# A decoder layer on one core: weights stored in four parts, score copies shared by two engines, and extra products on TensorE in the first batch

## The chip, the cores and the metric

The kernel runs on one core of one Trainium2 chip. The metric is device time in microseconds, the median of several executions. The core has a matrix engine (PE, with its weight loads shown as PEld), a vector engine (DVE), a scalar engine (ACT), GpSimd (POOL) and a sync engine (SP). Each engine takes its own instructions in their order and waits on semaphores where it needs another one's result. SP, ACT and POOL also issue transfers (SPq, ACTq, POOLq in the profile). Matrix results go to PSUM, from which DVE or ACT must copy them before anything else can use them.

## The reference: what is computed

Eight batches of 512 tokens by 256 channels in float32 pass through one decoder layer:

```python
x = _layernorm(x + attn(x))                  # banded self-attention, 16 heads of 16 channels
x = _layernorm(x + xattn(x, ctx, ctx))       # causal cross-attention
x = _layernorm(x + ffn(x))                   # 8 experts, the best 2 for each token
# attn:
q = _ln(silu(x @ Wq)); k = _ln(silu(x @ Wkv)[..., :C]); v = silu(x @ Wkv)[..., C:]
wp = silu(x @ Wwin + bwin)                   # gives a width and a sharpness per token and head
scores = stack([einsum('blhd,blhd->blh', q, k_pad[:, w:w+L]) for w in range(17)]) * SCALE
soft_mask = sigmoid((width - rel) * sharp)
attn = softmax(scores - (1.0 - soft_mask) * 1e4)
out = silu(sum(attn[..., w] * v_pad[:, w:w+L] for w in range(17)) @ Wout)
```

Every token sees 17 neighbours in the self-attention. The experts are two matrices with a gelu between them, 256 to 1024 to 256 channels.

## The kernel before

**Stages.** The work on a batch falls into three streams. `scores(b)` makes the projections, the layer norms of q and k, and the raw scores. `attended(b)` does the softmax, the weighted sum of values and the output projection. `crossed(b)` does the cross-attention and the routing to experts. The main loop runs from -2 to 8 and lays `crossed(b)`, `attended(b + 1)` and `scores(b + 2)` beside each other, so in the first round there is only `scores(0)`, in the second `scores(1)` and `attended(0)`, and in the third all three. From the fourth round on, tiles of the experts (`experts`) fill in: one tile in the fourth round, eight in the fifth, and so on. A function called `together` interleaves the streams by the amounts that they yield. From this, the framework's scheduler sets an order for PE, DVE, ACT and POOL by its own estimate of durations, so an edit at one place can move other instructions on those engines. The order on SP is that of the program.

**Scores (lines 309 to 430).** The batch is transposed on PE (line 248) and copied to `xT` by ACT (257). For each of four 128-token tiles PE makes two projections: `pa` (q and k, line 321) and `pb` (v and the window inputs, line 322). ACT copies them out through a silu (323, 324), and DVE adds the bias of the window inputs to `wp` (325). `wp` passes ACT twice (328, 334), goes to DRAM (335) and comes back in another layout as `ws` (POOL, 395), from which DVE builds the mask input `pen` (474, 485, 491) and ACT its sigmoid (492). Meanwhile q and k are normed (342 to 356), transposed (367) and copied to `qT` and `kT` (372, 378).

Then PE makes the scores `pq` (line 413) in four groups: two halves of the channels (c) by two pairs of token tiles (ip). A group has 16 products into four PSUM buffers, one per row group r. ACT copies the four buffers into `row` (421), which has two buffers, and issues two transfers of `row` to the DRAM tensor `band[c]` (425). The scores of half c come back as `s[c]` in the layout of one token quadruple per partition (`read_scores`, line 387, on POOL).

```python
                for r in range(HG):
                    nc.scalar.copy(row[:, :, r], pq[r])
```

**Weighted sums of the first three batches (`summed`, lines 495 to 588; `BANDED` is 3).** For each half c: DVE adds `pen` to `s` (518), takes the maximum (525) and subtracts it (526), ACT takes the exponential (529), and DVE sums and divides (531 to 533). The weights then go to the DRAM tensor `aband[c]` in one transfer (537) from SP: partition p holds tokens 4p to 4p + 3, in pieces of 136 bytes. They come back by groups of 128 tokens (`fetch`, 506, two transfers each, into two buffers `arow`). Group g reads the tokens that partitions 32g to 32g + 31 stored. PE transposes a group (`paT`, 575), DVE and ACT copy it to `aT` (579), PE multiplies it with the values (`pw`, 553), and ACT and DVE put the halves together in `oT` (562, 563). For c = 0 the first two fetches stand right behind the store on SP; each later one waits until PE has read the group two before it. From the fourth batch on another routine (`weighted`) does this part on DVE.

**The rest that the prediction speaks of.** `py` (595) is the output projection and `y` its silu (603). The norm that follows ends in DVE's `off` (292) and four scalings on ACT (295). In the cross-attention the transposes of `xr` and `c` give `x1T` and `cT` (248, 257); the scores `ps` (711), the softmax (718 to 727), the transposes `pt` (700) and the sums `po` (685) follow in steps. `route` ends in eight scatters to `sorted_x` (815) from POOL. An expert tile starts with the load `xs` from `sorted_x` (942, SP), which waits for all scatters of the batch, and its transpose `pxs` (997) on PE.

Of the kernel before, what the change touches and what calls it, by code (L numbers as in the profile page):

```python
# [8 lines left out]
F32 = mybir.dt.float32  # L9
# [5 lines left out]
P = 128  # L15
L = 512
E = 256
# [3 lines left out]
W = 17  # L21
# [4 lines left out]
HG = HH // 2  # L26
LINE = HG * SPAN * 2
HALO = W // 2
T = L // P
# [8 lines left out]
BANDED = 3  # L38
# [6 lines left out]
def decoder_layer_kernel(  # L45
# [16 lines left out]
    nc = tc.nc  # L62
# [4 lines left out]
    last = N // TS  # L67
# [10 lines left out]
    ps_h = ctx.enter_context(tc.tile_pool(name="ps_h", bufs=2, space=PSUM))  # L78
# [15 lines left out]
    wall = cpool.tile([P, KC, 3 * E + 2 * H], F32, name="wall")  # L94
# [4 lines left out]
    ident = cpool.tile([P, P], F32, name="ident")  # L99
# [75 lines left out]
    scattered, adds, out_of, read, turns, urgent = [], [], {}, [], [], []  # L175
# [112 lines left out]
    def layernorm(a, last=False, by=None):  # L288
# [4 lines left out]
        for j in range(T):  # L293
# [5 lines left out]
            else:  # L299
# [2 lines left out]
                    ALU.mult, ALU.add,  # L302
                )

    def scores(b, xb):


# [7 lines left out]
        for t in range(T):  # L315
            pa = ps_m.tile([P, 2 * E], F32, tag="m", name="pa")
            pb = ps_m.tile([P, E + 2 * H], F32, tag="m", name="pb")
            for kc in range(KC):
                lhs = xT[:, kc, t * P : (t + 1) * P]
                se = dict(start=(kc == 0), stop=(kc == KC - 1))  # L320
                nc.tensor.matmul(pa, lhs, wall[:, kc, 0 : 2 * E], **se)  # L321
                turns.append(nc.tensor.matmul(pb, lhs, wall[:, kc, 2 * E :], **se))  # L322
            nc.scalar.activation(qk[:, t, :], pa, AF.Silu)  # L323
            nc.scalar.activation(v[:, t, :], pb[:, 0:E], AF.Silu)
            nc.vector.tensor_tensor(wp[:, t, :], pb[:, E:], bwin_sb, ALU.add)  # L325
            yield 0.8
        yield 8.4
        nc.scalar.activation(wp, wp, AF.Silu)
        for c in range(2):
# [54 lines left out]
        def read_scores(c):  # L384
            lines = band[c].rearrange("(p t n) -> p t n", p=P, t=T)[:, :, 0:LINE]
            read.append(
                nc.gpsimd.dma_start(  # L387
                    s[c].rearrange("p t r w u -> p t r (w u)"),
                    lines.rearrange("p t (r n) -> p t r n", r=HG)[:, :, :, 0 : 2 * W],
                )  # L390
            )
# [9 lines left out]
        for c in range(2):  # L401
            s.append(apool.tile([P, T, HG, W, 2], F32, tag="s", name="s", bufs=3))
            for ip in range(T // 2):
                row = apool.tile([P, 2, HG, SPAN, 2], F32, tag="row", name="row", bufs=2)
                pq = [
                    ps_m.tile([P, 2, SPAN, 2], F32, tag="m", name=f"pq{r}") for r in range(HG)
                ]
                for ii in range(2):
                    for u in range(2):
                        at = (2 * ip + ii) * P + u * QB  # L410
                        for r in range(HG):
                            rs = slice(32 * r, 32 * r + 32)
                            nc.tensor.matmul(  # L413
                                pq[r][u * QB : (u + 1) * QB, ii],
                                qT[rs, c, at : at + QB],
                                kT[rs, c, :, at : at + SPAN].rearrange("p u k -> p k u"),
                                start=True,
                                stop=True,
                            )
                for r in range(HG):  # L420
                    nc.scalar.copy(row[:, :, r], pq[r])  # L421
                to = band[c].rearrange("(b n) -> b n", b=L // QB)[:, 0 : QB * LINE]
                to = to.rearrange("(i u) (p n) -> u p i n", u=2, n=LINE)
                for u in range(2):
                    nc.scalar.dma_start(
                        to[u, :, 2 * ip : 2 * ip + 2],
                        row[u * QB : (u + 1) * QB].rearrange("p i r k u -> p i (r k u)"),
                    )
                yield 2.0

                if c == 1 and ip == 0:
                    read_scores(0)
# [48 lines left out]
        for c in range(2):  # L481
            pc = pen[:, c].rearrange("p t r w u -> p (t r) w u")
            wc = width[:, c].rearrange("p t (r u) -> p (t r) u", u=2)
            sc = sharp[:, c].rearrange("p t (r u) -> p (t r) u", u=2)
# [11 lines left out]
    def summed(b):  # L496


        groups = [(c, g) for c in range(2) for g in range(T)]
        rows_of = {}  # L500

        def fetch(c, g):
            ar = apool.tile([P, HG, SPAN, 2], F32, tag="a", name="arow", bufs=2)
            for u in range(2):
                ub = (g * P + u * QB) * (LINE + 2)
                nc.sync.dma_start(
                    ar[u * QB : (u + 1) * QB].rearrange("p r k u -> p (r k u)"),
                    aband[c][ub : ub + QB * LINE].rearrange("(p n) -> p n", p=QB),
                )
            rows_of[c, g] = ar  # L510

        s, pen, vh = out_of.pop(b)
        for c in range(2):
            sc = s[c]


            with tc.issue_after(urgent[-1].ins) if urgent and c == 0 else nullcontext():
                nc.vector.scalar_tensor_tensor(
                    sc, pen[:, c], -4.0e4, sc, ALU.mult, ALU.add
                )  # L520
            flat = sc.rearrange("p t r w u -> p (t r) w u")
            byw = sc.rearrange("p t r w u -> p (t r) u w")
            full = [P, T * HG, W, 2]
            top = spool.tile([P, T * HG, 2], F32, tag="top", name="top")
            nc.vector.tensor_reduce(top, byw, AX.X, ALU.max)
            nc.vector.tensor_tensor(
                flat, flat, top[:, :, None, :].to_broadcast(full), ALU.subtract
            )
            nc.scalar.activation(sc, sc, AF.Exp, scale=0.25)
            den = spool.tile([P, T * HG, 2], F32, tag="den", name="den")  # L530
            nc.vector.tensor_reduce(den, byw, AX.X, ALU.add)
            nc.vector.reciprocal(den, den)
            nc.vector.tensor_tensor(
                flat, flat, den[:, :, None, :].to_broadcast(full), ALU.mult
            )
            lines = aband[c].rearrange("(p t n) -> p t n", p=P, t=T)[:, :, 0:LINE]
            nc.sync.dma_start(
                lines.rearrange("p t (r n) -> p t r n", r=HG)[:, :, :, 0 : 2 * W],
                sc.rearrange("p t r w u -> p t r (w u)"),
            )  # L540
            if c == 0:

                for early in groups[:2]:
                    fetch(*early)
            yield 5.0
        oT = apool.tile([P, KC, L], F32, tag="T", name="oT", bufs=4)
        aT = apool.tile([P, 2, HG, 2, P], F32, tag="prod", name="aT")

        def sums(c, g):
            po = ps_o.tile([P, 2, 2, QB], F32, tag="o", name="pw")  # L550
            for u in range(2):
                for r in range(HG):
                    nc.tensor.matmul(
                        po[32 * r : 32 * r + 32, u],
                        vh[c][0:SPAN, 2 * g + u, 32 * r : 32 * r + 32],
                        aT[0:SPAN, g % 2, r, :, u * QB : (u + 1) * QB],
                        start=True,
                        stop=True,
                    )

            to = oT[:, c, g * P : (g + 1) * P].rearrange("c (u q) -> c u q", u=2)
            nc.scalar.mul(to, po[:, :, 0, :], par[:, 0:1])
            nc.vector.scalar_tensor_tensor(
                to, po[:, :, 1, :], par[:, 1:2], to, ALU.mult, ALU.add
            )

        for k, (c, g) in enumerate(groups):
            if 2 <= k + 1 < len(groups):
                fetch(*groups[k + 1])
            ar = rows_of.pop((c, g))  # L570
            for i in range(2):
                pt = ps_h.tile([P, 2, 2, P], F32, tag="h", name="paT")
                for r in range(2):
                    for u in range(2):
                        nc.tensor.transpose(  # L575
                            pt[0:SPAN, r, u, :], ar[:, 2 * i + r, :, u], ident
                        )
                put = nc.scalar.copy if i else nc.vector.tensor_copy
                put(aT[0:SPAN, g % 2, 2 * i : 2 * i + 2], pt[0:SPAN])
            if k:  # L580
                sums(*groups[k - 1])
            yield 1.4
        sums(*groups[-1])
        yield 0.8
        return oT
# [616 lines left out]
```

## Time and profile before

| what | value |
|---|---|
| median of 3 runs | 1038.47 us (1036.89 to 1040.36) |
| the profiled execution's own time | 1045.55 us |
| its span, first to last instruction | 1043.8 us |
| mean granted clock of PE | 0.913 |
| PE busy over the span | 916.5 us (88%) |
| DVE, ACT, POOL busy | 627.4, 556.7, 251.5 us |
| 0 to 48 us (`scores(0)` alone) | PE 27.43 us busy, DVE 17.86, ACT 23.89, clock 0.77 |
| 48 to 107 us (second round) | PE 43.70, DVE 29.33, ACT 33.31, clock 0.76 |
| 107 to 204 us (third round) | PE 86.16, DVE 57.64, ACT 60.61, clock 0.80 |
| 204 to 300 us (fourth round) | PE 77.10, DVE 54.69, ACT 57.92, clock 0.79 |
| 300 to 1000 us (expert tiles) | PE 670.97, DVE 450.84, ACT 364.72, clock 0.98 |

The profile shows one execution. Times in a timeline are microseconds from the start of the span; its columns are start, duration, engine, line, operation, output and inputs, and in brackets the idle time of that engine before it with what ended it. The clock is the share of PE's full speed that it was granted. A group "x32" of PE in the timeline counts records: a float32 product shows as two records, a transpose as one. The bounds of the rounds are read off the timeline; the rounds overlap by a few us.

### The profile page before, as it was taken

The page shows a single profiled execution, that of the slowest core. Times are in us where ns is not written, and L with a number is a line of the kernel's source. Part 1 is how long each engine was busy: PE and PEld are TensorE (multiplying, and loading weights), DVE is VectorE, ACT ScalarE, POOL GpSimd, SP SyncE. Part 2 cuts the span into 40 slices and gives each one's busy share as a digit, 9 for nine tenths or more (in the row PEclk, how much of TensorE's full clock was granted, in tenths as well). Part 3 has the DMA queues.
Part 4 walks back from the last instruction along what each step waited for, and adds up shares of the span by engine and source line. Part 5 has one row for each costly group of instructions (what it writes and reads, how often), then busy time and mean ns, then how long its engine had stood idle before and what let it go on. Part 6 is the DMA issues. An engine that isn't in the chain of part 4 may idle for free. (4 is left out here: it accounts for less than half of the span.)

```text
span 1043.8 us, 18932 instructions
## 1 busy us (share of the span) xinstructions
PE 916.5 (88%) x6336; PEld 761.6 (73%) x6336; DVE 627.4 (60%) x2106; ACT 556.7 (53%) x978; POOL 251.5 (24%) x211
## 2 busy tenths in 40 slices
PE   5658879868979999999999999999999989999970
PEld 3435557546858777777888778887998988999960
DVE  5164654754489969979994989489953331111106
ACT  4556746656467556658755865576355311222224
POOL 1100100400232243125212522152241241121221
PEclk9677877867799989999999999999999999999995
DMA  9574563872699788689978896898898899999949
GB/s 205 137 124 135 115 153 81 227 164 64 185 319 311 239 267 271 198 257 337 282 206 268 309 292 184 234 364 292 264 279 256 272 260 372 314 337 323 330 116 320
DMA packets 129123, 252.09 MB, mean 242 GB/s; under 512 B 29536, under 2 KB 76704, under 8 KB 127744
## 3 DMA queue, kind: packets, MB, share of 16 engines
q1 hardware_dynamic: 89312, 183.30, 54.3%
q0 software_dynamic: 17824, 41.86, 16.2%
q10 hardware_dynamic: 21888, 25.70, 9.0%
q8 instruction: 52, 0.85, 0.3%
q14 instruction: 47, 0.39, 0.1%
HBM read 193.44 MB, written 57.36 MB: 240 GB/s over the span
## 5 line engine op out<-in xcount | busy, mean ns | idle before, releaser
L1011 PEld LDWEIGHTS ph<-xsT,w1h 128*128 128x128 f32 x2176 | 264.6, 196 | 14.2 <-issue 5.2
L1011 PE MATMUL ph<-xsT,w1h 128*128 128x128 f32 x2176 | 271.6, 280 | 2.9 <-DVE xsT L1000 2.8
L1028 PE MATMUL pf<-w2h,h 128*128 128x256 f32 x1088 | 255.9, 386 | 3.2 <-ACT h L1019 3.1
L1028 PEld LDWEIGHTS pf<-w2h,h 128*128 128x128 f32 x1088 | 204.1, 194 | 32.0 <-ACT h L1019 5.7
L1037 POOL DMA_INDIRECT total<-ye,toi x68 | 120.4, 1771 | 417.0 <-ACT ye L1036 117.0
L1019 ACT ACTIVATE h<-ph 128x512 f32<-128x512 f32 x136 | 81.2, 598 | 119.0 <-PE ph L1011 115.0
L1000 DVE COPY xsT<-pxs 128x256 f32<-128x256 f32 x68 | 28.7, 423 | 174.6 <-PE pxs L997 174.6
L651 DVE TENSOR_TENSOR prod<-prod 128x1024 f32<-128x1024 f32 (+3 forms) x160 | 104.1, 651 | 0.3
L1036 ACT ACTIVATE ye<-pf,g 128x256 f32<-128x256 f32 x68 | 32.2, 473 | 127.2 <-PE pf L1028 116.7
L643 DVE TENSOR_TENSOR prod<-vhalo,a 128x2176 f32<-128x2176 f32 x40 | 96.6, 2416 | 0.2
L815 POOL DMA_INDIRECT sorted_x<-xr,to x64 | 78.2, 1222 | 19.9 <-issue 17.1
L413 PE MATMUL pq<-kT,qT 32*64 32x160 f32 x1024 | 60.3, 391 | 19.2 <-ACT row L421 12.7
L387 POOL DMA_DIRECT2D s<-band x16 | 24.3, 1520 | 214.5 <-DMA band<-row 154.5
L321 PE MATMUL pa<-wall,xT 128*128 128x512 f32 x128 | 67.5, 615 | 6.0 <-ACT qk L323 4.7
L413 PEld LDWEIGHTS pq<-kT,qT 32*64 32x64 f32 x1024 | 37.2, 156 | 33.8 <-ACT row L421 18.1
L421 ACT COPY row<-pq 128x320 f32<-128x320 f32 x128 | 45.8, 435 | 29.4 <-PE pq L413 26.6
L575 PE MATMUL paT<-ident,arow 128*80 128x128 f32 x192 | 38.0, 346 | 20.0 <-DMA arow<-aband 17.1
L1019 ACT ACT_TABLE_LOAD x39 | 50.0, 1283 | 7.3 <-PE ph L1011 5.7
L322 PEld LDWEIGHTS pb<-wall,xT 128*128 128x128 f32 x128 | 24.2, 192 | 35.3 <-issue 23.0
L575 PEld LDWEIGHTS paT<-ident,arow 128*80 128x80 f32 x192 | 26.2, 167 | 30.8 <-issue 13.0
L711 PE MATMUL ps<-cT,x1T 128*128 128x128 f32 (+3 forms) x128 | 45.5, 476 | 0.0
L322 PE MATMUL pb<-wall,xT 128*128 128x288 f32 x128 | 41.3, 410 | 3.9 <-DVE wp L325 1.6
(196 smaller groups left out, 1392.4 us busy)
## 6 DMA issues: line engine op xcount, KB each, us to landing
w1h<-in_w_dram SPq DMA_DIRECT2D x136, 512.0 KB
w2h<-in_w_dram SPq DMA_DIRECT2D x136, 512.0 KB
band<-row ACTq DMA_DIRECT2D x64, 320.0 KB
vhalo<-vband POOLq DMA_DIRECT2D x10, 1280.0 KB, 10.1
xs<-sorted_x SPq DMA_DIRECT2D x68, 132.5 KB
arow<-aband SPq DMA_DIRECT2D x48, 160.0 KB
s<-band POOLq DMA_DIRECT2D x16, 272.0 KB, 5.8
xr<-in_x_dram SPq DMA_DIRECT2D x8, 512.0 KB
```

The costliest lines, as they stand in the source:

```text
L321: nc.tensor.matmul(pa, lhs, wall[:, kc, 0 : 2 * E], **se)
L322: turns.append(nc.tensor.matmul(pb, lhs, wall[:, kc, 2 * E :], **se))
L413: nc.tensor.matmul(pq[r][u * QB : (u + 1) * QB, ii], qT[rs, c, at : at + QB], kT[rs, c, :, at : at + SPAN].rearrange("p u k -> p k u"), st ...
L421: nc.scalar.copy(row[:, :, r], pq[r])
L575: nc.tensor.transpose(pt[0:SPAN, r, u, :], ar[:, 2 * i + r, :, u], ident)
L643: nc.vector.tensor_tensor(prod.rearrange("p w (h d) -> p w h d", d=D), vh[c][:, t : t + W, :].rearrange("p w (h d) -> p w h d", d=D), a[:, ...
L651: nc.vector.tensor_tensor(prod[:, 0:n, :], prod[:, 0:n, :], prod[:, n : 2 * n, :], ALU.add)
L815: sent = nc.gpsimd.indirect_dma_start(out=sorted_x[:, :], out_offset=bass.IndirectOffsetOnAxis(ap=to[:, n, j : j + 1], axis=0), in_=xr[:, ...
L1011: nc.tensor.matmul(ph[:, u, :], w1s[hf][:, kc, f * P : (f + 1) * P], xT[:, kc, :], start=(kc == 0), stop=(kc == KC - 1),)
L1019: nc.scalar.activation(h, ph, AF.Gelu)
L1028: nc.tensor.matmul(po, hs[fc // HU][:, fc % HU, j * P : (j + 1) * P], w2s[hf][:, f, :], start=(fc == 0), stop=(fc == NF - 1),)
L1037: add = nc.gpsimd.indirect_dma_start(out=total[:, :], out_offset=bass.IndirectOffsetOnAxis(ap=toi[:, j : j + 1], axis=0), in_=y, in_offset ...
```

## The change

It has three parts, and the order that the scheduler gives to PE, ACT and DVE in the first four rounds differs with them. The order on POOL is the same; SP has the added transfers and is otherwise the same. From the routing in the fourth round on, the order of every engine is the same as before.

1. The store of the weights of half c = 0 becomes four stores of 32 partitions each, so that a group's fetch depends on the one store that holds its tokens. The store of half c = 1 stays whole.
2. For the first three batches the four copies of a score group are shared: r = 0 and 2 on ACT, r = 1 and 3 on DVE.
3. In the first batch PE gets products that nothing reads: six of a 128x128 by a 128x512 operand behind the last projection, and one behind each score group.

```diff
+    def hold(n, behind):
+
+        none = ps_h.tile([P, 2 * E], F32, tag="h", name="none")
+        with tc.issue_after(behind.ins):
+            for _ in range(n):
+                nc.tensor.matmul(none, ident, wall[:, 0, 0 : 2 * E], start=True, stop=True)
...
             yield 0.8
+        if b == 0:
+            hold(6, turns[-1])
         yield 8.4
...
-                            nc.tensor.matmul(
+                            last = nc.tensor.matmul(
...
+                if b == 0:
+                    hold(1, last)
                 for r in range(HG):
-                    nc.scalar.copy(row[:, :, r], pq[r])
+                    put = nc.vector.tensor_copy if b < BANDED and r % 2 else nc.scalar.copy
+                    put(row[:, :, r], pq[r])
...
-            nc.sync.dma_start(
-                lines.rearrange("p t (r n) -> p t r n", r=HG)[:, :, :, 0 : 2 * W],
-                sc.rearrange("p t r w u -> p t r (w u)"),
-            )
+
+            parts = T if c == 0 else 1
+            for ps in (slice(k * P // parts, (k + 1) * P // parts) for k in range(parts)):
+                nc.sync.dma_start(
+                    lines[ps].rearrange("p t (r n) -> p t r n", r=HG)[:, :, :, 0 : 2 * W],
+                    sc[ps].rearrange("p t r w u -> p t r (w u)"),
+                )
```

## The prediction, made before the changed kernel was run

> **What bounds the kernel now.** First the busy shares of the page (PE 88%), then busy time by rounds. Columns: bounds, length, busy us of PE, PEld, DVE, ACT, POOL, clock, DMA share, GB/s.
>
> ```profile
> 0.00:48.00 48.00, 27.43 (x190) 18.17 (x191) 17.86 (x39) 23.89 (x45) 5.19 (x26) 0.77 0.73 168
> 48.00:107.00 59.00, 43.70 (x372) 27.71 (x371) 29.33 (x55) 33.31 (x62) 4.22 (x6) 0.76 0.63 134
> 107.00:204.00 97.00, 86.16 (x545) 59.10 (x546) 57.64 (x210) 60.61 (x118) 16.78 (x16) 0.80 0.56 133
> 204.00:300.00 96.00, 77.10 (x543) 56.06 (x541) 54.69 (x193) 57.92 (x108) 16.24 (x16) 0.79 0.62 174
> 300.00:1000.00 700.00, 670.97 (x4622) 590.53 (x4623) 450.84 (x1521) 364.72 (x615) 200.13 (x139) 0.98 0.89 282
> ```
>
> After 300 us PE is busy 671 of 700 at clock 0.98, and the order there is the same in both kernels, so a shift at 300 us arrives at the end one to one. Everything is decided before it, where chains leave PE idle 20.6, 15.3, 10.8 and 18.9 us a round at clocks below 0.8. The timeline shows the chains that the change touches:
>
> ```profile
> 36.10 1.11 ACT L492 ACTIVATE pen<-pen 128x1088 f32<-128x1088 f32 x1 [2.99 <-DVE pen L491]
> 37.12 1.39 ACT L421 COPY row<-pq 128x320 f32<-128x320 f32 x4
> 46.48 1.54 POOL L387 DMA_DIRECT2D s<-band  x1 [14.77 <-DMA band<-row]
> ...
> 57.83 0.60 SPq L537 DMA_DIRECT2D aband<-s  x1
> 67.19 2.44 SPq L506 DMA_DIRECT2D arow<-aband  x4
> 70.96 1.91 PE L575 MATMUL paT<-ident,arow 128*80 128x128 f32 x8 [7.49 <-DMA arow<-aband]
> 72.06 0.69 DVE L579 COPY aT<-paT 80x512 f32<-80x512 f32 x1 [4.17 <-PE paT L575]
> 72.67 0.18 DVE L325 TENSOR_TENSOR wp<-pb,bwin_sb 128x32 f32<-128x32 f32 x1
> 72.88 0.31 ACT L328 ACTIVATE wp<-wp 128x128 f32<-128x128 f32 x1 [5.77 <-DVE wp L325]
> ...
> 124.72 0.63 SPq L537 DMA_DIRECT2D aband<-s  x1
> 131.26 2.75 SPq L506 DMA_DIRECT2D arow<-aband  x4
> 136.01 0.84 PE L575 MATMUL paT<-ident,arow 128*80 128x128 f32 x3 [4.85 <-DMA arow<-aband]
> ...
> 210.12 0.67 SPq L537 DMA_DIRECT2D aband<-s  x1
> 217.51 2.40 SPq L506 DMA_DIRECT2D arow<-aband  x4
> 221.52 1.91 PE L575 MATMUL paT<-ident,arow 128*80 128x128 f32 x8 [3.08 <-DMA arow<-aband]
> ```
>
> Store to first fetch takes 9.36, 6.54 and 7.39 us, and PE, DVE and ACT all stand idle for it near 71. Windows on the second store:
>
> ```profile
> 124.70:126.00 1.30, 1.30 (x6) 0.72 (x5) 1.30 (x6) 1.14 (x2) 0.00 (x0) 1.00 0.00 0
> 126.00:128.40 2.40, 2.40 (x9) 1.29 (x8) 2.40 (x7) 2.32 (x6) 0.00 (x0) 1.00 0.85 116
> 128.40:131.20 2.80, 1.66 (x12) 1.13 (x10) 2.80 (x7) 1.68 (x5) 0.00 (x0) 1.00 0.00 0
> ```
>
> The DMA engines are idle 1.3 us, move 2.4, and are idle again for 2.9 until the fetch.
>
> **Part 1, the products.** A 128x512 product takes 0.86 us at full clock (starts of successive projections 9.73 and 10.59). Six behind the last projection (its end 19.3) take 5.2 us and end at 24.5, inside PE's 6.08 us of idle before the transposes of q and k at 25.38. At half clock they take 10.3, and the transposes start 4.2 late. Both are covered: the row copies wait on ACT behind the sigmoid of `pen` (36.10), which waits for a load that POOL can issue only at 30.92, while the first two groups end at 32.7. A clock kept up speeds the transposes (3.76 us for 16 records) by at most 1.9, for the same reason worth nothing. If the cover were gone, the six would cost 0 to 4.2. The single ones cost 0.86 or 1.72 each; behind the second group the wait of ACT for a free `row` (43.26) covers it, behind the last one PE goes to transposes that `xT` on ACT needs. Together 0 to 0.65, I take 0.3.
>
> **Part 2, the copies.** Four copies of a group take 1.39 to 1.41 us on ACT; two take 0.75 (another row of the trace has that pair). DVE's 128x320 copy from PSUM is not in the trace; the nearest rows are 128x256 in 0.42 and 80x512 in 0.69, so about 0.5 each, 1.0 the pair, 0.85 to 1.4 as bounds. PSUM buffers come free two at a time, so PE's third group of 16 products (37.58) can start some 0.6 to 1.0 earlier, and each of the two remaining groups saves 0.4. DVE idles there (17.86 of 48 busy). The read of `s` at 46.48 moves up by about 1.3; minus the 0.3, first round **-1.0** (0 to -1.5). Later rounds: DVE is busy 29 of 59 and 58 of 97, ACT 33 and 61; a copy waits behind whatever DVE does, so I take nothing, bounds -0.6 to +0.6 a round.
>
> **Part 3, the stores.** SP issues four transfers for one: 4 x 0.63 = 2.5 us, 1.9 more, while SP only waits for the fetch, whose first part needs the first store alone. By the windows, part 0 needs 1.3 us to its first packet, a quarter of 2.4 = 0.6 moving, and 0.7 to 2.9 to be seen: 2.6 to 4.8. I take 4.0, since the end looks like latency; gain 2.5 (1.7 to 3.9) per store, for the first of 9.36 more, to about 5. The later groups wait for two `arow` buffers, so they are not bound by parts 2 and 3 (issued 1.3 and 1.9 later). The second half's store, 69.80, queues behind the fetches on SP and moves with them.
>
> A price for splitting, beside the row: the Trainium skill, page "DMA: Bandwidth & Descriptors", section "Rules for kernel authors", says to coalesce, since under 64 KB one mostly pays overhead; the parts are 68 KB. By its fit in "Anatomy of one DMA" (2.0 us and bytes over 436,000, for another issue path) whole and part differ only 2.6 to 2.2 us: my estimate by that page is 0.5 per store. The row here, 6.5 to 9.4 us for the whole, is far above that fit, so the measurement decides; the rule is rival 1.
>
> **What follows in each round**, with the changed order of the instructions.
> - Second (48 to 107). The order puts `wp` of the last tile and the norms of q and k ahead of the first `aT` copy on DVE, so the `scores(1)` chain no longer waits for the fetch: `wp` 72.67 to about 66.8, the first row copies 96.48 to 90.5, the read of `s` 106.36 to 98.7. Of that 1.0 is round one, the store about 3, and the rest the reordering: **-7.0** (-2.5 to -8). If `wp` were still behind `aT`, only the -3 is left.
> - Third (107 to 204). The store at 124.72 moves to about 115.6. PE's idle 4.85 before 136.01 is filled with the scores and sums of the cross-attention, which the new order puts ahead of `paT`. Against it: ACT does `y2`, `cT`, `xT` ahead of the exponential, about 1.4. Then PE is the limit (22.41 of 24 us at 145 to 169, 20.32 of 21 at 169 to 190), so what was idle is the whole gain: **-1.5** (0 to -4). The load `xs` at 209.67, behind the scatters, would come at about 200.
> - Fourth (204 to 300). PE's order now has `pxs` (211.84, waits for `xs`) ahead of the transposes of `xr` that ran at 204.38; queued behind it are `x1T`, `ps` and `paT`. That costs about 2.8 (transposes 1.97, a copy 0.58), and the store here gives 2.5 of PE's 3.08 idle before 221.52: **0** (-0.4 to +2.8).
>
> Sum: -1.0 -7.0 -1.5 + 0 = **-9.5**. The profiled execution took 1045.55 (span 1043.8 and 1.75 around it), 7.1 above the median; it becomes 1036.05, and the median 1038.47 becomes **1029.0**.
>
> **Rivals.**
> 1. *Only the stores help, or little of them.* If a part takes as long as the whole, the latency being fixed, the stores give about 0; the reordering near 72 is what remains, -4.5 in all: 1034. For it: 2.9 of 6.54 us pass with idle DMA engines. Against: 6.54, 7.39 and 9.36 differ, so something grows with load.
> 2. *The clock stays up.* Two half-clock stretches lie before 300:
>
> ```profile
> 145.00:169.00 24.00, 22.41 (x216) 16.18 (x215) 20.83 (x62) 17.56 (x36) 0.02 (x1) 0.99 0.32 94
> 169.00:190.00 21.00, 20.32 (x169) 15.44 (x170) 4.11 (x22) 12.69 (x28) 2.21 (x2) 0.51 0.63 151
> 248.00:275.00 27.00, 25.17 (x235) 19.20 (x236) 4.85 (x22) 14.43 (x33) 2.01 (x2) 0.57 0.41 109
> ```
>
>    If filled gaps kept half of the 20 us from 169 at full clock, 5 more are saved: -14.5, 1024. The stretch was cold with PE busy 97%. The Trainium skill, page "TensorE: Matmul & The Clock Gate", Part 1, has the clock released after about 3.4 us of sustained activity and gated after an idle window; by that rule 169 to 190 would have been warm, which the row denies, so it earns only a small chance.
> 3. *Slower: the hot stretch goes cold.* The new order moves score products, transposes and router products, among which PE ran at half clock here, into the third round's filled gap, and 145 to 169 (22.41 us of PE at 0.99) may lose its clock. All of it cold adds 20 or so: 1038.47 - 9.5 + 20 = 1049. It decides from some 10 us of bound PE work turned cold. For it: clock changes come in blocks of 3.4 us whatever the busy share. Against: most of that stretch's work is 512 wide and unchanged.
> 4. *No change.* The lead is used up at the first barrier, the scatters to `xs`, or by 2.8 in the fourth round on top of a second round of -3: 1038. For it: barrier waits hide early finishes; against: the last scatter hangs on the same chain that moves up.
>
> **How the numbers follow.** Forecast 0.50 (its own range 1024 to 1033: the sums of the bounds, narrowed as they won't all fall together); rival 1 0.19, rival 2 0.10, no change 0.08, slower 0.13. About 0.3%, 3.1 us, is what a measurement here can tell from no change. Faster by more: 0.50 + 0.19 + 0.10 less 0.01 for rival 1's near edge = 0.78; same 0.09; slower 0.13. The range 1020 to 1037.5 leaves out the slower case and a part of no change, 2 in 10.
>
> **What would show it.** Six unread products end before 25.4; two DVE row copies a group, of about 0.5; the first fetch 4 to 5 us after its store's first issue; `wp` L328 no longer waiting some 5.8 us on DVE; `paT` waits near 71 and 136 shrunk by half or gone; `xs` issued near 200; PE from 300 on shifted by one number only. Wrong if fetches still come 6.5 us behind, if clocks in 107 to 300 fall below 0.79, or if `pxs` holds PE longer than 3 us more.

## The result and the profile after

The changed kernel was timed four times beside the kernel before. The lower the ratio, the faster the changed kernel.

| timing | changed, median | before, median | ratio, 95% interval |
|---|---|---|---|
| first, 22 executions of each | 1035.99 us | 1040.86 us | 0.9957 [0.9936, 0.9978] |
| `changed_again`, 12 against 35 | 1045.90 | 1050.46 | 0.9973 [0.9940, 1.0007] |
| `changed_third`, 6 against 18 | 1026.38 | 1038.34 | 0.9908 [0.9874, 0.9942] |
| `changed_fourth`, 12 against 23 | 1042.36 | 1047.56 | 0.9959 [0.9928, 0.9990] |

The ratio leaves out the executions in a slower state and is not the quotient of the two medians, which take in all.

Weighted by the inverse squares of the half widths the four give 0.9952, with a half width of 0.0014: about 5 us faster. The second and the third lie further apart than their intervals allow, so this half width is too small. Forecast were 9.5 us, 0.0091. The sign was right and the size twice too large. The kernel before timed against itself gave 0.9976 [0.9938, 1.0015] (`before_third`), so differences of two or three thousandths between two runs below mean little.

The profiled execution of the changed kernel took 1032.45 us, its span is 1030.8. Against the profile of before that is 13.1 us less, more than twice the difference of the medians: one pair of profiles does not give the size of this change. Busy time by rounds in the changed kernel (columns as in the prediction):

```profile
0.00:48.00 48.00, 37.73 (x214) 20.09 (x215) 21.36 (x47) 21.85 (x38) 5.95 (x26) 0.86 0.72 172
48.00:107.00 59.00, 42.74 (x385) 29.07 (x384) 32.70 (x63) 33.00 (x57) 5.04 (x6) 0.80 0.73 151
107.00:204.00 97.00, 77.82 (x531) 52.29 (x529) 67.63 (x226) 61.26 (x111) 16.52 (x16) 0.88 0.57 136
204.00:300.00 96.00, 80.26 (x599) 60.31 (x600) 60.35 (x209) 58.01 (x111) 16.18 (x17) 0.89 0.70 196
300.00:1000.00 700.00, 669.63 (x4633) 589.97 (x4631) 442.31 (x1502) 362.89 (x611) 201.52 (x140) 0.99 0.88 278
```

The third round is where the two differ most: PE is busy 8 us less in the same 97, at a clock of 0.88 and not 0.80, and DVE 10 us more. The timeline of the changed kernel, with the lines that answer to those of before (lines of the program are 7 to 15 higher now):

```profile
45.73 1.54 POOL L396 DMA_DIRECT2D s<-band  x1 [14.12 <-DMA band<-row]
56.88 2.74 SPq L552 DMA_DIRECT2D aband<-s  x4
64.31 2.41 SPq L518 DMA_DIRECT2D arow<-aband  x4
67.60 0.18 DVE L332 TENSOR_TENSOR wp<-pb,bwin_sb 128x32 f32<-128x32 f32 x1
67.81 0.31 ACT L337 ACTIVATE wp<-wp 128x128 f32<-128x128 f32 x1 [1.20 <-DVE wp L332]
68.75 3.77 PE L590 MATMUL paT<-ident,arow 128*80 128x128 f32 x16 [4.54 <-DMA arow<-aband]
70.69 1.34 SPq L518 DMA_DIRECT2D arow<-aband  x2
78.74 1.48 PE L590 MATMUL paT<-ident,arow 128*80 128x128 f32 x6 [4.15 <-DMA arow<-aband]
101.06 1.48 POOL L396 DMA_DIRECT2D s<-band  x1 [22.06 <-DMA band<-row]
...
118.55 2.63 SPq L552 DMA_DIRECT2D aband<-s  x4
121.55 3.67 SPq L518 DMA_DIRECT2D arow<-aband  x4
136.68 0.42 PE L590 MATMUL paT<-ident,arow 128*80 128x128 f32 x1 [2.94 <-DMA arow<-aband]
...
205.58 0.33 SPq L957 DMA_DIRECT2D xs<-sorted_x  x1
206.02 2.70 SPq L552 DMA_DIRECT2D aband<-s  x4
209.66 3.93 SPq L518 DMA_DIRECT2D arow<-aband  x4
```

The reader is to see three things. The fetch comes 7.43, 3.00 and 3.64 us after its store, not 9.36, 6.54 and 7.39. `wp` no longer waits for the fetch (1.20 us of idle ACT in front of it, 5.77 before). And PE waits 4.15 us in front of the third group's transposes at 78.74, whose fetch was issued at 70.69; before, that wait was shorter:

```profile
79.88 1.91 PE L575 MATMUL paT<-ident,arow 128*80 128x128 f32 x8 [1.71 <-DMA arow<-aband]
```

Since one profile is not enough, the table sets the mean of three profiles of the kernel before (the first, `again_before`, `before_third`) against that of four of the changed kernel. Times count from the issue of the first load of `ws` (28.6 to 30.9 us in these profiles), which nothing in the change precedes but the six products.

| landmark | before | changed | shift | forecast |
|---|---|---|---|---|
| read of `s`, first round | 15.6 us | 14.8 us | -0.8 | -1.0 |
| first store to its fetch | 8.7 | 6.9 | -1.8 | -4.4 |
| read of `s`, second round | 74.3 | 70.0 | -4.3 | -7.7 |
| second store | 92.8 | 87.4 | -5.4 | -9.1 |
| second store to its fetch | 6.5 | 3.0 | -3.5 | -2.5 |
| load `xs`, fourth round | 176.8 | 173.9 | -2.9 | -9.5 |
| third store to its fetch | 6.9 | 3.5 | -3.4 | -2.5 |
| copy `xsT` of the fifth round's first tile | 269.0 | 260.2 | -8.8 | -9.5 |
| last instruction | 1010.2 | 1004.7 | -5.5 | -9.5 |

At 300 us the forecast is nearly met, but by another way: less in the second round, a loss in the third, and 5.9 us in the fourth, where none was expected. The standard deviation between profiles of the changed kernel is 2.5 us at the second store, 3.6 at the fifth round and 8.4 at the end, so the last row is known worst.

### The profile page after: what moved, and what is told of

Its sections match the earlier page's. It is cut to its first block, busy times and chain, and to the rows that moved or that the text cites. A ratio compares the mean times of both kernels' runs of the same rounds, so it can differ in the third digit from the quotient of the medians.

```text
span 1030.8 us, 19002 instructions
## 1 busy us (share of the span) xinstructions
PE 908.2 (88%) x6356; PEld 751.7 (73%) x6356; DVE 640.4 (62%) x2130; ACT 549.6 (53%) x955; POOL 250.2 (24%) x211
## 5 line engine op out<-in xcount | busy, mean ns | idle before, releaser
L1015 DVE COPY xsT<-pxs 128x256 f32<-128x256 f32 x68 | 28.6, 421 | 177.2 <-PE pxs L1012 177.2
L422 PE MATMUL pq<-kT,qT 32*64 32x160 f32 x1024 | 57.5, 378 | 13.7 <-ACT kT L387 5.4
L422 PEld LDWEIGHTS pq<-kT,qT 32*64 32x64 f32 x1024 | 34.1, 150 | 31.7 <-ACT kT L387 10.4
L433 ACT COPY row<-pq 128x320 f32<-128x320 f32 x104 | 37.9, 433 | 28.8 <-PE pq L422 23.6
L590 PE MATMUL paT<-ident,arow 128*80 128x128 f32 x192 | 32.0, 309 | 15.6 <-DMA arow<-aband 12.2
L295 ACT ACTIVATE xr<-xr,off,rs 128x256 f32<-128x256 f32 x64 | 33.2, 593 | 22.1 <-DVE off L292 22.0
L700 PE MATMUL po<-c,prT 128*128 128x256 f32 x160 | 41.4, 390 | 3.8 <-ACT prT L719 3.7
## 6 DMA issues: line engine op xcount, KB each, us to landing
s<-band POOLq DMA_DIRECT2D x16, 272.0 KB, 6.5
```

The costliest lines, as they stand in the source:

```text
L422: last = nc.tensor.matmul(pq[r][u * QB : (u + 1) * QB, ii], qT[rs, c, at : at + QB], kT[rs, c, :, at : at + SPAN].rearrange("p u k -> p k u"),
L433: put(row[:, :, r], pq[r])
L700: nc.tensor.matmul(po, probsT[j][:, i * P : (i + 1) * P], c[:, i, :], start=(i == 0), stop=(i == j),)
```

## The experiments

Theory 1 was that of the prediction: stores and new order give the time, copies a little, products nothing. Theory 2 was that the products, by the clock, or the copies give it.

**Three profiles of the kernel before, and each part alone.** `again_before` is the kernel before, for a second profile. The three others undo two of the three parts.

> The kernel before, unchanged, for a second profile of it. Theory 1 (the two profiles can be set beside each other, and their 13.1 us are the change): read of s in the second round near 106.4, xs of the fourth round's tile at 209.7, xs of the fifth round at 299.6, each within 2 us; clock from 204 to 300 near 0.79. Theory 2 (a good part of the 13.1 us is the granted clock of the one execution that was profiled, since the medians differ by 4.9 only): xs of the fifth round comes 4 to 9 us earlier than in the first profile at a clock above 0.83 from 204 to 300, with the read of s in the second round unchanged.

One execution took 1037.36 us. From the first load of `ws` the read of `s` in the second round came after 73.6 us (75.4 in the first profile), the copy of the fifth round's first tile after 268.8 (272.0), at a clock of 0.78 from 204 to 300. Both theories were off. Counted so, the two profiles differ by 3 us at 300. Counted from the start of the span, as in the expectation, the load `xs` of the fifth round comes 4.9 us earlier, which is theory 2's shift, but 2.3 of them are there at the first load of `ws`, and the clock did not rise.

```diff
+            parts = T if c == 0 else 1
+            for ps in (slice(k * P // parts, (k + 1) * P // parts) for k in range(parts)):
-                nc.sync.dma_start(lines..., sc...)
+                nc.sync.dma_start(lines[ps]..., sc[ps]...)
```

> The kernel before with only the store of half c = 0 in four parts. Theory 1 (the stores and the order that follows carry the gain): store to fetch 5.0, 3.5, 3.6 us in place of 9.4, 6.5, 7.4, the read of s in the second round 3 to 7 us earlier, median 4 to 8 us less. Theory 2 (the products and the clock carry it): store to fetch as short, but at most 2 us less at the median, ratio within 0.002 of 1.

Ratio 0.9914 [0.9887, 0.9942] (1030.0 against 1037.56 us): 9 us by the ratio, 7.6 by the medians, where the whole was to give 9.5. Store to fetch 7.1, 2.9 and 3.3 us; the first was to be 5.0.

```diff
-                    nc.scalar.copy(row[:, :, r], pq[r])
+                    put = nc.vector.tensor_copy if b < BANDED and r % 2 else nc.scalar.copy
+                    put(row[:, :, r], pq[r])
```

> The kernel before with only the score copies of the first three batches shared by ACT and DVE. Theory 1: the read of s in the first round 1.0 to 1.3 us earlier, ratio 0.9985 to 1.0005. Theory 2: the same, nothing at the end. Rival: DVE delays other work in rounds two and three, ratio over 1.001.

Ratio 0.9962 [0.9931, 0.9993], 4 us: more than either theory had. The read of `s` in the first round came 0.8 earlier.

```diff
+        if b == 0:
+            hold(6, turns[-1])
...
+                if b == 0:
+                    hold(1, last)
```

> The kernel before with only the ten unread products. Theory 1: no gain, the row copies still start behind the sigmoid of pen at about 37.1, ratio 1.000 to 1.001. Theory 2: the clock of the first round rises from 0.77 to about 0.86 and stays higher up to 300, ratio 0.995 to 0.998.

Ratio 1.0032 [0.9999, 1.0066]: no gain, so the products do not carry it, although the clock of the first round rose as theory 2 had it. The first line is the first round of `products_only`, the second of `again_before`:

```profile
0.00:48.00 48.00, 38.51 (x217) 20.69 (x218) 17.86 (x39) 24.96 (x47) 5.97 (x26) 0.89 0.71 175
```

```profile
0.00:48.00 48.00, 29.61 (x194) 19.41 (x195) 17.86 (x39) 25.08 (x47) 5.98 (x26) 0.77 0.74 177
```

The read of `s` in the first round comes 15.6 us after the first load of `ws` in both. A higher clock was of no use there: that round waits for `ws`.

**Each part left out of the whole.**

> The changed kernel without its ten unread products. Theory 1 (the stores are worth about 8 to 9 us and the copies 1 to 4, as alone, and the products take 3 or more back): ratio 0.986 to 0.991. Theory 2 (stores and copies take the same idle time away, so that together they are worth little more than one; the products are near nothing): ratio 0.993 to 0.997.

> The changed kernel without the shared copies. Theory 1: stores less products, ratio 0.993 to 0.996. Theory 2: about as the stores alone, 0.989 to 0.993.

> The changed kernel with the store whole. Theory 1: copies less products, ratio 0.998 to 1.001. Theory 2: 0.995 to 0.997.

> The changed kernel, unchanged, on the same chip as its variants, and for a second profile. Both theories: ratio 0.994 to 0.998 as before. If the chip matters, nearer to 0.990.

| kernel | ratio, 95% interval |
|---|---|
| `no_products` | 0.9908 [0.9866, 0.9950] |
| `no_shared_copies` | 0.9976 [0.9936, 1.0016] |
| `whole_stores` | 1.0044 [1.0003, 1.0085] |
| `changed_again` | 0.9973 [0.9940, 1.0007] |

The stores are what counts: with them whole the rest is no gain (1.0044, against 0.9973 with them split). The copies, worth 4 us alone, add nothing to the stores: 0.9973 with them and 0.9976 without, and where the products are left out 0.9914 (three timings of `no_products`, below) and 0.9914 (`stores_only`). Every pair here and in the first set pointed to a price of the products, from 0.3 to 0.8%. That was odd, since the order of all other instructions on PE, DVE, ACT and POOL is the same with the products and without. So the next runs asked for its cause.

**Are the products dear?** `six_only` leaves out the single products, `ones_only` the six, and `narrow_products` makes them small; `no_products_2` and `no_products_3` repeat `no_products`; `products_even` takes six tiles from the pool and not five; `products_double` doubles the products.

```diff
 # narrow_products
-                nc.tensor.matmul(none, ident, wall[:, 0, 0 : 2 * E], start=True, stop=True)
+                nc.tensor.matmul(none[:, 0:8], ident, wall[:, 0, 0:8], start=True, stop=True)
-            hold(6, turns[-1])
+            hold(1, turns[-1])
 # products_even
-            hold(6, turns[-1])
+            hold(3, turns[-1])
+            hold(3, turns[-1])
 # products_double
-            hold(6, turns[-1])
+            hold(12, turns[-1])
-                    hold(1, last)
+                    hold(2, last)
```

> The changed kernel without the ten products, again, as the base of the three kernels beside it. In all theories ratio 0.988 to 0.994.

> The changed kernel with the six products behind the projections, without the four single ones. Theory P1 (the five tiles that the products take from the pool ps_h, an odd number, swap the two buffers for everything that follows): one tile, also odd, so 0.3 to 0.7% slower than without products. Theory P2 (the matrix work of the products costs later, by way of the clock): 0.2 to 0.5% slower. Theory P3 (the single products delay the score copies): 0 to 0.1% slower.

> The changed kernel with the four single products, without the six. P1: four tiles, an even number, as without products. P2: 0.1 to 0.3% slower. P3: 0.3 to 0.7% slower.

> The changed kernel with one product of 8 columns in place of the six and of each single one: five tiles of the pool as in the changed kernel, and next to no matrix work. P1: 0.3 to 0.7% slower than without products. P2: as without products. P3: as without products, or 0.1% slower.

> The changed kernel without the ten products, on one chip with the three beside it. All theories: ratio 0.988 to 0.994.

> The changed kernel, unchanged. P1 (odd number of tiles from ps_h) and P2 (the matrix work): 0.3 to 0.7% slower than without products. P0 (the products cost nothing and the earlier differences were of chip and chance): within 0.2% of it.

> The changed kernel with the six products as three and three on two tiles, so that six tiles instead of five come from ps_h; the same matrix work. P1: as without products. P2: as the changed kernel, 0.3 to 0.7% slower than without. P0: within 0.2%.

> The changed kernel with twelve products and two behind each group. P2: 0.7 to 1.3% slower than without products. P1: as the changed kernel. P0: the read of s of the first round 0 to 1.5 us later, and no more than that, 0 to 0.15%.

| one set | ratio | next set, same chip | ratio |
|---|---|---|---|
| `no_products_2` | 0.9923 [0.9886, 0.9961] | `no_products_3` | 0.9911 [0.9876, 0.9945] |
| `six_only` | 0.9946 [0.9909, 0.9983] | `changed_third` | 0.9908 [0.9874, 0.9942] |
| `ones_only` | 0.9918 [0.9884, 0.9953] | `products_even` | 0.9931 [0.9906, 0.9957] |
| `narrow_products` | 0.9941 [0.9903, 0.9979] | `products_double` | 0.9942 [0.9914, 0.9971] |

P1 falls: an even number of tiles (0.9931) is no better than an odd one (0.9908). Of P3 nothing is seen: with the single products alone (`ones_only`) the ratio is 0.9918, without any 0.9923. P2 as I had it falls too: twice the work was to cost 0.7 to 1.3% and cost 0.3. That is 3 us, and 3.0 are seen in the first round, where 20 products instead of none push the read of `s` back (`products_double`):

```profile
47.15 1.54 POOL L396 DMA_DIRECT2D s<-band  x1 [17.04 <-DMA band<-row]
```

It stands 17.8 us behind the first load of `ws`, 14.8 in `no_products_3`. P0 held in that set (0.9908 with the products, 0.9911 without) and not in that of `changed_again`. The three timings without products give 0.9914 with a half width of 0.0022 (weighted as above), the four with them 0.9952 with 0.0014. Between them lie 0.0038 with a half width of 0.0026, but side by side on a chip the difference was 0.0065 once and -0.0003 once. A cost of the products between nothing and 7 us stays open; no gain from them was found.

> The kernel before against itself, timed as the others, and a third profile of it. If the intervals given are to be believed, ratio 0.996 to 1.004. P0: a stray of 0.3% is common. At the first tile of the fifth round (the first expert tile that follows the routing of the second batch) its trace stands 6 to 10 us behind those of the changed kernel, counted from the first load of ws.

> The changed kernel again, on the chip of before_third. P0 (the products cost nothing; the gain is that of the stores and the new order, 0.7 to 0.9%, and the first result is on its low side): ratio 0.989 to 0.995. P2 (the products take half of it back): 0.994 to 0.998.

They gave 0.9976 and 0.9959. In `before_third` the first tile of the fifth round stands 6.1 us behind the mean of the four profiles of the changed kernel, as expected. The second ratio lies within P2's range, but the kernel before strayed nearly as far from itself, so this pair does not decide it. Versions faster than the kernel before, and by these timings not slower than the changed one, are `stores_only` (0.9914) and `no_products` (0.9914 over three timings).

## Why the prediction was half right

**What held.** The six products fit in front of the transposes of q and k. In the changed kernel's timeline they run from 19.33 to 24.64, and PE is idle another 0.93 us until q and k are ready:

```profile
19.33 5.31 PE L310 MATMUL none<-wall,ident 128*128 128x512 f32 x12
25.58 2.37 PE L376 MATMUL pt<-ident,qk 128*128 128x128 f32 x16 [0.93 <-DVE qk L365]
...
35.95 0.88 DVE L433 COPY row<-pq 128x320 f32<-128x320 f32 x2
```

The faster transposes (2.37 for 3.76 us) brought nothing, as costed. DVE's copies took 0.44 each, within my bounds of 0.42 and 0.69, and the first round gave -0.8 for -1.0. Store to fetch at the second and third store fell by 3.5 and 3.4 us, within the bounds of 1.7 and 3.9 and above the 2.5 that I took; rival 1, parts as slow as the whole, is wrong in its mechanism, though its time, -4.5, is what came out.

The Trainium skill, page "DMA: Bandwidth & Descriptors", section "Rules for kernel authors", speaks for one large transfer in place of several small ones. Here the four stores won, 0.7% beside `whole_stores`: the reader needs a quarter of the bytes first.

**Step that failed 1: the first store, "to about 5", and the later groups, "not bound by parts 2 and 3".** The first fetch came 6.9 us behind its store (mean). Transfers of GpSimd were on the DMA engines then: POOL issues the second read of `s` and a load of `vblock` 1 to 2 us ahead of this store (54.69 and 55.84). Windows in the changed kernel:

```profile
56.90:59.60 2.70, 2.70 (x5) 1.56 (x6) 1.47 (x4) 1.60 (x4) 0.03 (x1) 0.64 0.99 194
59.60:62.00 2.40, 2.40 (x6) 1.24 (x5) 1.78 (x3) 1.02 (x3) 0.00 (x0) 0.69 1.30 141
62.00:64.30 2.30, 2.21 (x7) 0.95 (x5) 2.30 (x6) 2.27 (x3) 0.00 (x0) 1.00 0.35 14
...
70.70:74.70 4.00, 3.88 (x40) 2.74 (x40) 2.76 (x5) 3.17 (x6) 0.00 (x0) 0.50 1.37 115
74.70:78.70 4.00, 0.00 (x0) 0.00 (x0) 0.26 (x1) 0.30 (x1) 0.27 (x1) 0.50 1.05 213
```

The share of the DMA engines is 0.99 and 1.30 in the first five us (above 1 where packets overlap), where the window on the second store of before that I worked from had 0.00 ahead of its packets. By queues (packets, MB, share of the engines), first from 56.9 to 59.6 us, then from 59.6 to 64.3:

```profile
q0 software_dynamic: 156, 0.52, 99.2%
```

```profile
q1 hardware_dynamic: 2111, 0.28, 72.8%
q0 software_dynamic: 36, 0.08, 9.9%
```

Queue q0 holds GpSimd's transfers, and the 0.28 MB on q1 are the four parts: all were issued before the first of their packets moved, 2.7 us behind the first issue, and they moved in one stretch. In `no_products_3` POOL issued the load of `vblock` 0.05 us behind the store instead of 1.04 ahead of it, and the fetch came after 4.61 us, the least of all. Yet the read of `s` in the second round stood at 70.2 us there, and at 70.0 in the changed kernel. So the shorter first fetch alone did not move the round there.

What it runs into is the next fetch. In the last two lines of the windows, from 74.70 to 78.70, PE does nothing and the engines are full while the third group's fetch is under way. PE's two waits for fetches took 7.49 and 1.71 us before and 4.54 and 4.15 now, 0.5 less in all (by the mean of the three and the four profiles, 7.5 before and 6.8 now). I had costed what the split store's part waits for, but not what the earlier fetches run into. With that, the second round gave -4.3 to the read of `s` where -7.7 was forecast (the sum took -8.0 for the two rounds). The reordering itself was as I had it: `wp` was at 67.60, forecast 66.8.

**Step 2: the third round, "-1.5".** From the second store on it gave +2.5: the lead of 5.4 us there is 2.9 at the load `xs`. The load waits for the scatters, and POOL now waits ahead of the first of them. DVE and ACT and POOL, before:

```profile
186.13 0.24 ACT L795 ACTIVATE ex<-ex 128x4 f32<-128x4 f32 x1
186.40 0.17 DVE L797 TENSOR_SCALAR inv<-ex 128x4 f32<-128x4 f32 x1 [2.21 <-ACT ex L795]
...
192.14 0.74 DVE L807 COPY xr<-token 128x4 f32<-128x4 f32 x1
...
193.92 1.08 POOL L815 DMA_INDIRECT sorted_x<-xr,to  x1 [0.30 <-issue]
```

and in the changed kernel:

```profile
185.68 0.20 ACT L810 ACTIVATE ex<-ex 128x4 f32<-128x4 f32 x1
186.83 1.49 POOL L396 DMA_DIRECT2D s<-band  x1 [10.80 <-DVE upto L866]
187.51 0.71 DVE L530 SCALAR_TENSOR_TENSOR s<-pen,s 128x544 f32<-128x544 f32 x1
188.26 0.72 DVE L537 TENSOR_REDUCE top<-s 128x32 f32<-128x544 f32 x1
189.04 0.72 DVE L538 TENSOR_TENSOR s<-s,top 128x544 f32<-128x544 f32 x1
189.67 0.68 DVE L620 TENSOR_TENSOR xr<-xr,y 128x512 f32<-128x512 f32 x1
190.28 0.16 DVE L812 TENSOR_SCALAR inv<-ex 128x4 f32<-128x4 f32 x1
190.81 0.18 DVE L815 TENSOR_TENSOR xr<-oh,inv 128x32 f32<-128x32 f32 x1
191.50 0.16 DVE L822 COPY xr<-token 128x4 f32<-128x4 f32 x1
192.59 1.08 POOL L830 DMA_INDIRECT sorted_x<-xr,to  x1 [3.52 <-ACT qk L330]
```

The router's `ex` is ready 0.49 us earlier, and before it was used 0.03 us after its end. Now DVE's order has ahead of `inv` small operations that plan the experts, up to 187.5, and then four large ones of the next batch's softmax and output, so that it starts 4.40 us after `ex` ended; the columns of `xr` that the scatters read are written at 191.66, and POOL starts 0.93 later after an idle time of 3.52. (The profile names an activation of ACT as the releaser; the copy on DVE is the last write to `xr` before it.) The read of `s` ahead of the scatters had come 4.6 us earlier, the scatters come 1.3 earlier. I had read DVE's new order only for the second round. Rival 4 had named the scatters as the place where a lead is used up, but took it that the last scatter hangs on the chain that moves up. This wait comes with the shared copies. It is 2.87 to 3.52 us in all profiles of kernels that have them (the changed kernel four times, `copies_only`, `no_products` and eight more), and 0.30, the distance of issue, in all six without: the kernel before three times, `products_only`, `stores_only` and `no_shared_copies`. `copies_only` and then `stores_only`:

```profile
195.34 1.08 POOL L816 DMA_INDIRECT sorted_x<-xr,to  x1 [3.52 <-ACT qk L323]
```

```profile
189.50 1.08 POOL L817 DMA_INDIRECT sorted_x<-xr,to  x1 [0.30 <-ACT xT L257]
```

From the second store to the first scatter the six without shared copies took 65.9 to 70.5 us and the fourteen with them 72.6 to 78.2. That the copies add nothing beside the stores is in keeping with it, and so is the second round, where the two parts gain the same time: the read of `s` stood at 71.4 us with the copies alone, at 71.4 with the stores alone and at 71.0 with both (mean of three, without products). That this is the whole reason was not tried.

**Step 3: the fourth round, "0".** From the load `xs` to the copy of the fifth round's first tile the mean fell from 92.2 to 86.3 us. The order with `pxs` ahead of the transposes was as forecast, and those ran at 208.24, 3.9 later than before. Against that, the third store gave its fetch 3.4 us. The rest, 2.5, is not settled, but it goes with the order that the shared copies bring: `copies_only` and `whole_stores`, with no split store, were at 84.9 and 86.0 in the same stretch, `products_only` at 92.7; the split stores without shared copies gave 87.1 (`stores_only`) and 89.2 (`no_shared_copies`). From the second store to the fifth round's first tile the two kinds of order come out alike, 171 to 177 us with shared copies and 172 to 178 without, so what they lose at the scatters they win back here. How, was not tried.

**Step 4: "passes through one to one".** The lead at the fifth round was 8.8 us and at the end 5.5, with a standard deviation of 8.4 among the four ends, so this is not shown to be false. It is what separates -8.8 from the -5 of the timings, and it is where the open cost of the products would have to lie.

**The clock**, rival 2: from 204 to 300 the first two profiles had 0.79 and 0.89, but `again_before` had 0.78, `stores_only` 0.82 and `copies_only` 0.89, with nearly the same place of the fifth round's first tile (263.1 and 263.4). So the clock there is not what the parts differ by; whether it is part of why the first pair of profiles is 13.1 us apart is not shown. Rival 3 did not come at its price: by rounds the clock of the changed kernel was above that of before (0.88 for 0.80, 0.89 for 0.79). But the stretch from 145 to 169 that it named had 0.86 for 0.99, and the one from 169 to 190, which was cold before, 0.76 for 0.51.

## What to carry to other kernels

Where a fetch needs a part of what one store writes, splitting the store pays even though each part has a latency of its own: 6.5 us came down to 3.0 where the queues were quiet, and to 6.9 of 8.7 where they were not, so look at what else is on the DMA engines in that window, and at whether the next fetch then becomes the wait. If an edit lets a scheduler reorder an engine, read the new order as far as the next barrier: operations moved ahead of one of 0.16 us on DVE made POOL wait 3.5 us ahead of the scatters, where it had been 0.3. Time the parts alone and left out before keeping them together, and take several profiles of both kernels where one execution differs from the next by as much as the change is worth.

## What the hardware showed beside that

In three of the five sets of timings behind the first one the kernel before took 1047.56 to 1051.20 us, in the two others 1037.56 and 1038.34. The chip does not decide it: one chip gave 1050.46, 1051.20 and 1038.34, the other 1037.56 and 1047.56. About half of that lies at one place. From the copy `xsT` of the 47th expert tile to that of the 48th it takes 7.1 or 7.2 us in all profiles of the two sets, and 12.1 to 14.9 us in all of the three, whatever the kernel. There all engines stop together, as in `changed_fourth`:

```profile
842.78 0.27 PE L1012 MATMUL pxs<-ident,xs 128*128 128x128 f32 x1 [1.15 <-issue]
845.81 1.09 ACT L1034 ACTIVATE h<-ph 128x512 f32<-128x512 f32 x2 [6.11 <-remote]
845.96 0.42 DVE L1015 COPY xsT<-pxs 128x256 f32<-128x256 f32 x1 [8.88 <-remote]
```

PE's product ends at 843.05 and DVE takes it up 2.9 us later, with nothing of the data flow between them. What holds them was not tried.
